# The first image's four chunks of x, loaded in halves of 64 channels instead of halves of 512 columns

## The chip, the core and the metric

The kernel runs on one core of one Trainium2 chip. The core has TensorE (matrix products, PE in the profile, with its weight loads shown apart as PEld), VectorE (DVE), ScalarE (ACT), GpSimd (POOL) and SyncE (SP, which here only issues transfers). Transfers between the memory of the chip (HBM) and the core's on-chip memory (128 partitions) are issued by SP, ACT or POOL, each on a queue of its own, and are carried out by 16 DMA engines that all queues share.

The metric is the time of one execution in microseconds on the device. The kernel before takes 3139.58 us, the median of three runs that lie between 3139.58 and 3139.60 us.

## What is computed

The input x has 16 images of 512 channels by 32 x 32 pixels, in float32. For every image: a group normalisation over 8 groups of 64 channels, a 1 x 1 convolution to queries, keys and values, attention with 4 heads of 128 channels over the 1024 pixels, a 1 x 1 convolution of the result, and the sum with x.

```python
b, c, h, w = x.shape                                   # 16, 512, 32, 32
xg = x.reshape(b, NUM_GROUPS, -1)                      # 8 groups
mu = jnp.mean(xg, axis=-1, keepdims=True)
var = jnp.var(xg, axis=-1, keepdims=True)
xn = ((xg - mu) * jax.lax.rsqrt(var + EPS)).reshape(b, c, h, w)
xn = xn * norm_gamma[:, None, None] + norm_beta[:, None, None]
qkv = jnp.einsum('oc,bchw->bohw', qkv_w, xn) + qkv_b[:, None, None]
q, k, v = jnp.split(qkv, 3, axis=1)
q, k, v = (to_heads(q), to_heads(k), to_heads(v))      # 4 heads of 128
attn = jax.nn.softmax(jnp.einsum('bhnd,bhmd->bhnm', q, k) * scale, axis=-1)
out = jnp.einsum('bhnm,bhmd->bhnd', attn, v)
out = out.transpose(0, 1, 3, 2).reshape(b, c, h, w)
out = jnp.einsum('oc,bchw->bohw', proj_w, out) + proj_b[:, None, None]
return x + out
```

## The kernel before, in words

An image is held as four chunks of 128 channels by 1024 pixels: the channels lie on the partitions, and a chunk is 512 KB. The products with the weights are done by Strassen's scheme (seven products of blocks instead of eight, for queries and keys on two levels), so that a chunk is used in blocks of 512 columns: b11 and b12 are the left and right halves of the upper two chunks, b21 and b22 those of the lower two. The images are pipelined: while the attention of one image runs, the statistics, the normalisation and the products of the next one are placed between its matrix products. Only the first image has nothing in front of it, and its work up to the first product is written out by hand in `open_image`.

The order at the start, by line:

- `load_x(0)` (L227 to L237, called at L240) issues the first transfers of the program. For each of the four chunks SP loads the left 512 columns and ACT the right 512 columns, so each queue issues four transfers of 128 rows of 2 KB. Images after the first are loaded by POOL, one transfer of 128 rows of 4 KB for each chunk.
- `stage_v` (L490 to L505) then makes SP load the weights of the values: a11, a21, a22 and a12, two transfers of 128 KB each. They use the same eight semaphores as the transfers of x, one after the other, so each of them is issued only when the x transfer that had its semaphore has landed. Further weights (`load_block`, L380; L434) follow on SP.
- TensorE starts with small products of constants (`warm`, L1263 to L1268) that no result uses. They stand at three places between the steps of the statistics.
- The statistics of the upper two chunks are made on VectorE (`chunk_steps`, L44 to L54): `bn_stats` (L49) of the left half, of the right half, and `bn_aggr` (L52). Two products with a matrix of averages (L82 and L87), some small steps on VectorE and a power on GpSimd (L89) give scale and shift for the groups of these two chunks (L76, L1293).
- Then the upper chunks are normalised in place, half by half (`apply`, L104 to L111): the left halves on VectorE (L111), the right halves on ScalarE (L108). The first product of the program's result, p1 of the values (`v_units`, L839 to L848), needs the left halves of both upper chunks and a11. Its result is copied by ScalarE (L565).
- ScalarE makes the statistics of the third chunk (L1303 to L1307) as soon as it is there, VectorE those of the fourth (L49 again). The lower chunks are normalised later (L1355 to L1358).
- The sums of the scheme follow on VectorE: t1 = b12 - b11 for each of the upper chunks and s1 = a21 + a22 (L1284), which the next product, p5, needs.

The instructions of the opening are kept in the order of the program where `keep_in_program_order` is called on them; the others are placed by a planner, which estimates when their operands are there.

Of the kernel before, what the change touches and what calls it, by code (L numbers as in the profile page):

```python
# [16 lines left out]
P = 128  # L17
# [4 lines left out]
HALF = 512  # L22
# [163 lines left out]
def fast_path(ctx, tc, x, sources, out, consts, flag, dims):  # L186
# [7 lines left out]
    B, C, N, NCC, NH2, NB, GC, SCALE = dims  # L194
# [29 lines left out]
    xs, xb, vs, qs, ks, os_, ob = {}, {}, {}, {}, {}, {}, {}  # L224
    mvs, scaled = {}, {}

    def load_x(b, chunks=range(NCC)):  # L227
        for c in chunks:
            xs[b, c] = xpool.tile([P, N], F32, tag="x", name=f"x_{b}_{c}")
            for half in range(NH2 if b == 0 else 1):  # L230
                i = ts(half, HALF) if b == 0 else ds(0, N)

                eng = nc.gpsimd if b > 0 else nc.scalar if half == 1 else nc.sync
                dma = eng.dma_start(xs[b, c][:, i], x[b, ts(c, P), i])
                if b > 0:

                    tc.keep_in_program_order(dma)  # L237


    load_x(0)  # L240
    primer = one.tile([BLK, 1], F32, name="primer")
    nc.vector.memset(ones, 1.0)
# [709 lines left out]
    def where(s):  # L952
        bh, j = divmod(s, NB)
        return (*divmod(bh, HEADS), j)
# [232 lines left out]
    def plan_head(b, h):  # L1187
# [3 lines left out]
        if h == 0:  # L1191
            if b > 0:
                products(plan, staggered(next_qk.pop()), NB)
                plan[6].append(lambda: o_blocks(b - 1))
                plan[6].append(lambda: sums_of_b(ob[b - 1]))
            else:
                products(plan, staggered(next_qk.pop(), (0, 4, 8, 12)), 0)
                plan[1].append(beside["second head"])
                plan[3].append(lambda: load_x(1, range(KC)))
                for c in range(KC):  # L1200
                    for half, step in enumerate(stats_steps(1, c)):
                        plan[4 + 2 * c].append(lambda step=step: behind_exp(step))
        elif h == 1:
            if b > 0:
                products(plan, staggered(proj_groups(b - 1), (0, 4, 8, 13)), NB, "proj")
            if b + 1 == B:
                plan[0].append(lambda: last_loads("x"))
            else:
                chunks = range(NCC) if b > 0 else range(KC, NCC)
                plan[0].append(lambda: load_x(b + 1, chunks))  # L1210
                at = (2, 4) if b > 0 else (1, 3)
                spread(plan, [lambda c=c: stats_chunk(b + 1, c) for c in chunks], *at)
                gather, scale = stats_group(b + 1)
                if b == 0:
                    plan[3].append(gather)
                    plan[4].insert(0, scale)
                else:
                    plan[4].insert(0, gather)
                    plan[5].insert(0, scale)
                for r in range(2):  # L1220
                    units = [
                        lambda c=c, half=half: normalise(b + 1, c, half, b > 0 or c % 2 == 1)
                        for c in range(KC * r, KC * r + KC) for half in range(NH2)
                    ]
                    plan[5 + r] += units if b > 0 else [
                        lambda u=u: behind_exp(u) for u in units
                    ]
                plan[6].append(lambda: x_sums(b + 1, (1,)))
# [159 lines left out]
    for s in range(steps + 1):  # L1388
        units = []
        if s < steps:  # L1390
            b, h, j = where(s)
# [175 lines left out]
```

## Time and profile before

| what | value |
|---|---|
| median of 3 runs | 3139.58 us (3139.58 to 3139.60) |
| the profiled execution | 3139.65 us |
| its span, first to last instruction | 3137.9 us |
| TensorE busy | 3129.2 us (100% of the span) |
| VectorE / ScalarE / GpSimd busy | 2658.0 / 1446.3 / 512.2 us |
| granted TensorE clock, mean over the span | 0.999 |
| issue of the eight x transfers of image 0 | 0.76 to 2.61 us |
| first product of the result (p1 of the values) | starts at 11.14 us |

Times within the profile are microseconds from the first instruction of the program. Busy time is the time in which an engine had an instruction under way. The chain that ended last follows the work back from the last instruction, at each step to what released it. A transfer is issued at one time and lands later; it has landed when all of its 16 parts have counted up its semaphore.

### The profile page before, as it was taken

The page shows a single profiled execution, that of the slowest core. Times are in us where ns is not written, and L with a number is a line of the kernel's source. Part 1 is how long each engine was busy: PE and PEld are TensorE (multiplying, and loading weights), DVE is VectorE, ACT ScalarE, POOL GpSimd, SP SyncE. Part 2 cuts the span into 40 slices and gives each one's busy share as a digit, 9 for nine tenths or more (in the row PEclk, how much of TensorE's full clock was granted, in tenths as well). Part 3 has the DMA queues.
Part 4 walks back from the last instruction along what each step waited for, and adds up shares of the span by engine and source line. Part 5 has one row for each costly group of instructions (what it writes and reads, how often), then busy time and mean ns, then how long its engine had stood idle before and what let it go on. Part 6 is the DMA issues. An engine that isn't in the chain of part 4 may idle for free.

```text
span 3137.9 us, 34036 instructions
## 1 busy us (share of the span) xinstructions
PE 3129.2 (100%) x10400; PEld 2197.3 (70%) x10400; DVE 2658.0 (85%) x4665; ACT 1446.3 (46%) x2653; POOL 512.2 (16%) x922
## 2 busy tenths in 40 slices
PE   9999999999999999999999999999999999999999
PEld 7567777777777777777777777777777777777764
DVE  8988889788897888978799787997879978799785
ACT  3545435354354543545435453453534545344433
POOL 0121121111211112111121101212012120121200
PEclk9999999999999999999999999999999999999999
DMA  5554554545545455454555545555455554555631
GB/s 177 169 193 148 197 172 165 164 152 191 172 169 165 146 198 172 162 168 148 194 170 170 169 143 189 174 172 172 142 183 172 178 183 134 183 162 182 191 118 48
DMA packets 209692, 522.21 MB, mean 166 GB/s; under 512 B 32336, under 2 KB 65488, under 8 KB 209504
## 3 DMA queue, kind: packets, MB, share of 16 engines
q1 hardware_dynamic: 131360, 277.34, 28.7%
q0 software_dynamic: 65184, 207.75, 19.5%
q10 hardware_dynamic: 12960, 34.87, 3.3%
q8 instruction: 86, 1.41, 0.2%
q14 instruction: 102, 0.84, 0.1%
HBM read 386.67 MB, written 133.17 MB: 166 GB/s over the span
## 4 chain that ended last, share of the span: by engine, by line
PE 100%; DMA 0%; DVE 0%; issue 0%; SPq 0%
PE po L1033 28%; PE s L960 28%; PE qk_x L687 12%; PE qk_y L687 9%; PE v_x L687 6%; PE pp_x L687 6%; PE pp_y L687 4%; PE v_y L687 4%; PE v_x L841 0%; PE lx L1119 0%; PE v_y L841 0%; PE ly L1119 0%; DMA x<-in_x 0%; PE v_z L841 0%; PE lz L1119 0%; PE warm L1267 0%
## 5 line engine op out<-in xcount | busy, mean ns | idle before, releaser
L960 PE MATMUL s<-qk,qk 128*128 128x512 f32 x2048 | 1045.9, 592 | 0.2 <-DVE qk L823 0.2
L1033 PE MATMUL po<-p,v 128*128 128x512 f32 x2048 | 1045.5, 592 | 0.0
L966 ACT ACTIVATE p<-s 128x512 f32<-128x512 f32 x1024 | 610.4, 596 | 877.7 <-PE s L960 859.2
L1033 PEld LDWEIGHTS po<-p,v 128*128 128x128 f32 x2048 | 616.3, 301 | 375.1 <-issue 258.0
L979 DVE TENSOR_TENSOR tot<-tot,p 128x1024 f32<-128x1024 f32 x385 | 469.4, 1219 | 142.2 <-ACT p L966 141.0
L960 PEld LDWEIGHTS s<-qk,qk 128*128 128x128 f32 x2048 | 389.0, 190 | 70.9 <-issue 14.6
L687 PEld LDWEIGHTS qk_x<-qk_t,w 128*128 128x128 f32 x1344 | 254.5, 190 | 153.3 <-issue 95.5
L687 PE MATMUL qk_x<-qk_t,w 128*128 128x256 f32 x1344 | 353.4, 380 | 0.0
L565 ACT COPY qk_u<-qk_x 128x512 f32<-128x512 f32 (+1 forms) x256 | 136.3, 532 | 238.0 <-PE qk_x L687 238.0
L892 POOL DMA_DIRECT2D vd<-vu x120 | 66.4, 553 | 958.9 <-DVE vu L884 958.9
L712 DVE TENSOR_TENSOR qk_r<-qk_y,qk_u 128x512 f32<-128x512 f32 (+1 forms) x256 | 157.7, 616 | 34.2 <-ACT qk_u L565 21.8
L943 POOL DMA_DIRECT2D out_y<-y x120 | 65.1, 543 | 645.5 <-DVE groups L300 401.3
L712 DVE TENSOR_TENSOR v_r<-v_y,v_u 128x512 f32<-128x512 f32 (+1 forms) x120 | 75.7, 631 | 107.7 <-ACT v_u L565 77.4
L687 PE MATMUL pp_x<-pp_t,w_proj 128*128 128x256 f32 x630 | 165.4, 379 | 0.0
L687 PE MATMUL v_x<-v_t,w_v 128*128 128x256 f32 x630 | 165.4, 379 | 0.0
L661 POOL DMA_DIRECT2D kept_t<-qk_t x240 | 129.6, 542 | 216.3 <-DVE qk_t L655 190.2
L687 PEld LDWEIGHTS pp_x<-pp_t,w_proj 128*128 128x128 f32 x630 | 119.7, 190 | 62.5 <-issue 35.9
L687 PEld LDWEIGHTS v_x<-v_t,w_v 128*128 128x128 f32 x630 | 119.7, 190 | 59.0 <-issue 34.4
L897 POOL DMA_DIRECT2D v<-vd x240 | 140.0, 590 | 65.5 <-issue 36.8
L687 PE MATMUL qk_y<-x,w 128*128 128x256 f32 x512 | 142.1, 379 | 0.0
L823 DVE SCALAR_TENSOR_TENSOR qk<-qk_r,qkb_sb,qk_r 128x512 f32<-128x512 f32 x192 | 137.4, 745 | 1.7
L884 DVE STREAM_TRANSPOSE vu<-vt 128x512 f32<-128x512 f32 x120 | 135.3, 1128 | 0.2 <-DMA vd<-vu 0.2
(229 smaller groups left out, 4395.1 us busy)
## 6 DMA issues: line engine op xcount, KB each, us to landing
w<-kept SPq DMA_DIRECT2D x90, 512.0 KB, 3.9
kept_t<-qk_t POOLq DMA_DIRECT2D x180, 256.0 KB, 2.7
v_t<-kept_t SPq DMA_DIRECT2D x180, 256.0 KB, 2.8
w<-kept SPq DMA_DIRECT2D x90, 384.0 KB, 3.4
rinv<-row ACTq DMA_DIRECT2D x63, 512.0 KB, 4.8
x<-in_x POOLq DMA_DIRECT2D x60, 512.0 KB, 4.8
vd<-vu POOLq DMA_DIRECT2D x120, 256.0 KB, 2.8
v<-vd POOLq DMA_DIRECT2D x240, 128.0 KB, 4.0
```

What stands on the lines that cost most here:

```text
L565: nc.scalar.copy(t[n][:, :width], t["x"][:, :width])
L661: nc.gpsimd.dma_start(t, to)
L687: latest["product"] = nc.tensor.matmul(acc[:, ts(i, Q)], have["w"][t][:, i, slot, :], inner(i, bn), start=(first and i == 0), stop=True, s ...
L712: latest["outer"] = nc.vector.tensor_add(dst, view(a), view(c))
L823: return nc.vector.scalar_tensor_tensor(st[b, h][:, ts(half, HALF)], a, qkb_sb[:, i : i + 1], c, ALU.add, ALU.add)
L884: nc.vector.transpose(u.rearrange("p (q i j) -> p j q i", q=n, i=BLK), t.rearrange("p (j q i) -> p j q i", q=n, i=BLK),)
L892: nc.gpsimd.dma_start(rows[which][ts(h, P), :], u)
L897: nc.gpsimd.dma_start(vs[b, pair][ts(q, BLK), half].rearrange("m h (k i) j -> m (h k) (i j)", k=n), rows[which].rearrange("(k m) (q e) -> ...
L960: latest["score"] = nc.tensor.matmul(sc, ks[b, h][:, ts(j, P)], qs[b, h][:, ts(half, HALF)], start=True, stop=True)
L966: exps[s] = nc.scalar.activation(ps[s][:, ts(half, HALF)], sc, AF.Exp, scale=SCALE)
L979: added[b, h, j] = nc.vector.tensor_add(tot[b, h][:, i], tot[b, h][:, i], ps[s][:, i])
L1033: summed = nc.tensor.matmul(po[half], v_block(b, h, j), ps[s][:, i], start=(j == 0), stop=(j == NB - 1),)
```

## The change

The transfers of image 0 are cut the other way: SP loads channels 0 to 63 of each chunk and ACT channels 64 to 127, all 1024 columns. Each queue still issues four transfers of 256 KB, now 64 rows of 4 KB on 64 partitions instead of 128 rows of 2 KB on 128 partitions. Images after the first are loaded as before.

```diff
             for half in range(NH2 if b == 0 else 1):
-                i = ts(half, HALF) if b == 0 else ds(0, N)
+                i = ts(half, P // 2) if b == 0 else ds(0, P)
 
                 eng = nc.gpsimd if b > 0 else nc.scalar if half == 1 else nc.sync
-                dma = eng.dma_start(xs[b, c][:, i], x[b, ts(c, P), i])
+                dma = eng.dma_start(xs[b, c][i, :], x[b, ts(c, P), :][i, :])
```

An instruction that reads a half of the columns of a chunk, on all 128 partitions, had one transfer to wait for and now has two. In the instruction streams this shows at the left-half `bn_stats` of the first, second and fourth chunk (L49), at the right-half normalisations on ScalarE (L108) and at the first products that read a chunk. The order of the instructions is the same on TensorE, VectorE, GpSimd and SP. On ScalarE one pair changes places: the copy of p1 (L565, `v_0_p`) now stands ahead of the normalisation of the second chunk's right half (L108) instead of behind it:

```
 L108 Activation x_0<-x_0,sh,sc 128x512
+L565 TensorCopy v_0_p<-v_0_x 128x512
 L108 Activation x_1<-x_1,sh,sc 128x512
-L565 TensorCopy v_0_p<-v_0_x 128x512
 L565 TensorCopy v_1_p<-v_1_x 128x512
```

## The prediction

> **What bounds the kernel now.** I read the page first, then the chain that ended last in its first 16 us, then the waits, the stretches and the transfers there. The page:
>
> ```profile
> PE 3129.2 (100%) x10400; PEld 2197.3 (70%) x10400; DVE 2658.0 (85%) x4665; ACT 1446.3 (46%) x2653; POOL 512.2 (16%) x922
> PE 100%; DMA 0%; DVE 0%; issue 0%; SPq 0%
> ```
>
> TensorE is busy from end to end and is the chain. The change leaves its 10400 products alone, so the end can only move if the first real product (p1, line 841) starts at another time, or if TensorE later waits. What sets p1 is the opening (start us, length us, what):
>
> ```profile
> 0.76 0.39 SPq L234
> 1.15 0.06 issue
> 1.21 4.83 DMA x<-in_x
> ...
> 6.06 1.30 DVE st L49 x2
> ...
> 7.38 0.22 DVE mv L52
> ...
> 7.64 0.40 PE pm L82 x2
> ...
> 8.66 0.38 PE pv L87 x2
> 9.05 2.12 PE warm L1267 x18
> 11.16 2.41 PE v_x L841 x10
> ```
>
> The chain begins with the second chunk's left-half transfer, which lands at 6.03; the statistics start at 6.06, the average at 7.64. From 9.05 to 11.14 TensorE is filled with products of constants, but the real chain there is ve, the power on GpSimd, scale, shift and the normalisation (VectorE, to 11.09), after which p1 starts at 11.14. So what the second chunk gains or loses at 6.06 goes 1:1 to p1, and as TensorE is never idle after it, 1:1 to the end.
>
> A second chain ends close by: p1 needs a11, which SP loads behind x.
>
> ```profile
> SPq L503 <- DMA x<-in_x: 4.1, 4, 1.9
> DVE st L49 <- DMA x<-in_x: 3.1, 2, 2.9
> ACT junk L1303 <- DMA x<-in_x: 3.7, 1, 3.7
> ```
>
> By the trace's landings, the SP transfers of x land at 4.32, 6.03, 7.61 and 8.97, ACT's at 4.49, 6.22, 7.86 and 9.16; a11 lands at 9.44 and 9.81 (1.3 us before p1), a21 and a22 by 11.25 (their sum s1 starts at 13.71). How busy the transfers are, by stretch (last column GB/s):
>
> ```profile
> 4.50:6.00 1.50, 1.50 (x15) 1.50 (x15) 1.34 (x3) 0.00 (x0) 0.00 (x0) 1.00 1.02 378
> 6.00:7.50 1.50, 0.28 (x3) 0.09 (x1) 1.41 (x3) 0.00 (x0) 0.00 (x0) 1.00 1.06 396
> ```
>
> All 16 engines are full (share 1.02 and 1.06), so x arrives at the engines' rate and any change of that rate shows.
>
> **The change, part by part.**
>
> *Issue.* The eight transfers take 0.39 to 0.45 us each to issue. Transfers with 128 contiguous rows of 4 KB took 0.32 us (weights from the kept store, line 425) to 0.36 us (last image's x, line 1085). So 0.06 to 0.1 us less ahead of each; the second chunk's landing is set by the engines, so I count 0.07 us once at most.
>
> *Larger packets.* Packets of 2048 bytes take 84 ns on an engine, packets of 4096 bytes 159 ns (the trace's medians on the hardware queues). Up to the second chunk each engine moves 32 of the small ones, 2.69 us, or 16 of the large, 2.54 us: 0.14 us earlier if nothing else changes.
>
> *Waiting for both halves.* The first statistics of a chunk now need both transfers. For the second chunk the later one counts: 6.22 instead of 6.03, so +0.19 us. For the first chunk 4.49 instead of 4.34: its statistics would end at 6.03 instead of 5.88, just ahead of the second's start, nothing. These three together: 6.22 - 0.14 = 6.08, or 6.01 with the faster issue, against 6.03: -0.02 to +0.05 us.
>
> *64 partitions per transfer.* The trace has no 64-partition transfer of this kind. The nearest rows are the value blocks v<-vd, 128 KB onto 32 partitions each. In 245 to 246 us they run alone:
>
> ```profile
> q0 software_dynamic: 78, 0.20, 95.7%
> v<-vd POOLq DMA_DIRECT2D x3, 128.0 KB, 4.7
> ```
>
> 95.7% of 16 engines over 1 us is 15.3 us; less the 29 small packets at 9 ns each, 49 packets of 4 KB took 307 ns each, nearly twice 159, and 0.20 MB a us is half of the 378 to 396 GB/s above. Landings of these blocks come 0.7 us apart, those of the 128 KB weight transfers onto 128 partitions 0.36 us. Part of it may be their 512-byte pieces (27 ns each, eight make 216 ns), so the row bounds the cost from above. From below: here two queues work on the two disjoint halves at once, and engines that take turns could keep all partitions busy, which costs nothing (159 ns). I take the middle, 1.5 x 159 = 239 ns: both queues begin together, 0.2 us apart at most, so the engines start in step on the same half, but nothing holds them in step.
>
> The landing of chunk c (0 to 3) is 0.76 + 2.39 + 8 p (c + 1), p the packet time; 2.39 us is what the first chunk shows over its sixteen 84 ns packets (4.49 - 0.76 - 1.34). The next chunk came 0.39 us later than this rule; at the slower rate I let that be absorbed.
> - p = 159 ns: as computed above, 6.08.
> - p = 239 ns: second chunk 6.97, fourth 10.8. Statistics start at 7.0 instead of 6.06: +0.95. a11's first piece comes 0.28 us behind ACT's fourth transfer (9.44 - 9.16), so 11.1, its second 0.37 later; p1 at 12.1. The weights are no bound.
> - p = 318 ns: second chunk 8.24, +2.2 by the statistics; fourth 13.3, a11 at 13.6 and p1 there: +2.5. Now the weights set it.
>
> *Clock.* TensorE idles from 6.29 to 7.64 now (1.36 us) and keeps the clock. At the end of the program the last product ends at 3132.40 and the recorded clock halves at 3134.53, after 2.1 us. With +0.95 the gap is 2.3 us, so the clock may halve before line 82; at the start it took from 1.45 to 4.51 to be granted in full. The 22 constant products would then run at 213 instead of 112 ns, and would still be running when p1 is ready: line 82 at 8.6, full clock at about 11.7, by then 8 of the last 18 are done, the other 10 take 1.1 us, p1 at 12.8 instead of 12.1. Between 0 and +0.7 us; I take 0, since both times are near the edge.
>
> *SP, ACT and what stands behind.* SP's weight transfers wait for the x landings and come later by what x loses (fourth chunk +1.6 at 239 ns, +4.1 at 318): a22 at 11.25 + 4.1 = 15.4 against s1 at 13.71 + 2.5 = 16.2, covered; the query weights land by 16.65 and are read at 25.25, covered. ScalarE's copy of p1 now stands ahead of the second chunk's right half: that normalisation moves from 11.3 to 13.77 and ends at 14.55, while its reader t1 starts at 14.84 after other VectorE work. Free, with 0.3 us of cover; VectorE would pass any overrun to p5 (14.98) 1:1, bounded by the 0.58 us of the copy. The additional waits on PE, DVE and ACT are a semaphore instruction each (17 ns where the trace shows them), on queues that stand idle then.
>
> *Sum.* Profiled execution 3139.65 (span 3137.9 and 1.75 around it), 0.07 us over the median: 3139.58 + 0.95 + 0.0 (issue, packets and both halves are inside the landings) + 0 (clock) = 3140.5 us.
>
> **The rivals.**
>
> A. *The halves overlap in full* (p = 159 ns): -0.02 to +0.05 us, 3139.6 us; at best 3139.4, if packets and issue gain and ACT's half no longer trails. For it: the two queues together cover all 128 partitions. Against it: v<-vd.
>
> B. *The halves take turns* (p = 318 ns): +2.5 us and up to +0.9 for the clock, whose gap is then 3.5 us: 3142.1 to 3143.0. For it: v<-vd at 307 ns. [...]
>
> C. *Slower by more than 0.2%, through a11.* p1 waits for a11, which queues on SP behind x. This decides from p1 = 11.14 + 6.3 = 17.4, a11 at 17.4 and the fourth chunk at 17.1: p = (17.1 - 3.15) / 32 = 436 ns, 2.7 times the row of 159 and 1.4 times the slowest sustained row (307). With B's clock at half for three more microseconds of products (+1.5) it is 3144.5, still inside. Single 4 KB packets over 436 ns exist, only beside other queues' traffic. Time: 3146 and more.
>
> D. *Faster by more than 0.2%* would need 6.3 us of the 11.14 before p1; x would have to land before it is issued. Practically out.
>
> **How the numbers follow.** 0.2% (6.3 us) is about what a measurement can tell from no change. Middle case 0.38, A 0.29, B 0.27, C 0.05, D 0.01. The likeliest is the middle, 3140.5. The range runs from A's best, 3139.4, to B with its clock, 3143.0, and leaves out C, D and little else. Faster 0.01, slower C's 0.05 and 0.01 for what B might add; the rest, 0.93, is within 0.2%.
>
> **What would show it.** Second chunk's statistics starting at about 7.0 (A: 6.05, B: 8.3); packets of 4 KB on the SP and ACT queues at 240 ns (159, 318); DMA rate in 4.5 to 7.5 us near 270 GB/s (390, 205); p1 at 12.1 (11.1, 13.7), released by VectorE's normalisation in the middle case, by a11 in B; t1 of the second chunk still right behind its VectorE predecessor. I am wrong if p1 moves by over 0.3 us while the packets stay at 159 ns, or if the end moves otherwise than p1.

## The result, and the profile after

The changed kernel takes 3144.17 us (median of 22 runs, 3142.93 to 3145.12) against 3139.62 us for the kernel before (22 runs, 3139.42 to 3140.24): a ratio of 1.0014, 95% interval 1.0008 to 1.002. That is 4.5 us slower, within the 0.2% named in the prediction, but outside its range, which ended at 3143.0. The profiled execution took 3144.00 us with a span of 3142.2 us (before 3139.65 and 3137.9).

The page shows the same bound as before; TensorE's 10400 products take 2.8 us more:

```profile
PE 3132.0 (100%) x10400; PEld 2200.2 (70%) x10400; DVE 2658.4 (85%) x4665; ACT 1446.1 (46%) x2653; POOL 512.3 (16%) x922
```

The chain that ended last in the changed kernel, first 18 us (start us, length us, what):

```profile
0.76 0.60 SPq L234
1.36 0.06 issue
1.42 6.67 DMA x<-in_x
...
8.18 1.30 DVE st L49 x2
...
9.76 0.59 PE pm L82 x2
10.35 1.06 PE warm L1267 x4
11.41 0.22 PE pv L87 x2
11.63 4.05 PE warm L1267 x18
15.68 2.29 PE v_x L841 x10
```

The statistics of the second chunk start at 8.18 instead of 6.06 us (+2.12). But p1 starts at 15.47 instead of 11.14 (+4.33; the chain's 15.68 is the end of the last constant product). So more than half of the loss does not come from the late x. Two things lie between. The first normalisation (line 111) starts at 13.13 instead of 10.54, that is +2.59: the two averaging products (0.59 instead of 0.40 us, and one that has to wait for the constant products ahead of it) cost 0.47 us. The normalised half is there at 13.68, and a11 landed at 12.27 and 12.60, yet the 18 constant products take 4.05 instead of 2.12 us and occupy TensorE until 15.5: another 1.74 us. The sum 2.12 + 0.47 + 1.74 is 4.33. The last product of the program ends at 3136.67 instead of 3132.39, +4.28: nothing is won back or lost later.

Why the constant products are slow is seen in stretches of 3.41 us, cut at the recorded changes of the clock (5.58, 8.99 and 15.82 us) and once between them (busy us of PE, PEld, DVE, ACT, POOL with counts, then the granted TensorE clock, DMA share, GB/s):

```profile
2.17:5.58 3.41, 3.41 (x18) 3.41 (x17) 0.00 (x0) 1.49 (x2) 0.36 (x1) 1.00 1.02 245
5.58:8.99 3.41, 1.22 (x11) 1.02 (x9) 2.31 (x5) 0.00 (x0) 0.00 (x0) 1.00 1.06 242
8.99:12.41 3.42, 2.65 (x12) 2.65 (x13) 1.39 (x7) 1.33 (x3) 0.49 (x1) 0.50 1.04 288
12.41:15.82 3.41, 3.41 (x17) 3.40 (x16) 3.00 (x9) 1.97 (x4) 2.10 (x4) 0.50 1.02 287
15.82:19.23 3.41, 3.41 (x18) 3.00 (x17) 2.03 (x8) 1.30 (x2) 0.00 (x0) 1.00 0.85 229
```

TensorE was idle from 6.79 to 9.76. The clock was halved at 8.99 and came back only at 15.82, two stretches of 3.41 us later. In the kernel before, stretches of the same length, cut from its recorded change at 4.51 us, give:

```profile
1.09:4.51 3.42, 3.06 (x14) 3.06 (x15) 0.39 (x3) 1.49 (x2) 1.22 (x2) 1.00 0.71 218
4.51:7.92 3.41, 2.05 (x19) 1.86 (x17) 2.82 (x6) 0.04 (x1) 0.00 (x0) 1.00 1.04 385
7.92:11.33 3.41, 3.32 (x26) 2.96 (x27) 1.84 (x10) 3.34 (x7) 2.00 (x4) 1.00 1.00 319
```

There TensorE was busy for 60% of the stretch with the gap, and the clock stayed. (The first rows of both tables show 1.00 because no clock is recorded before its first change; the first products there run 213 ns apart, as at the granted 0.50, against 112 ns after the change.)

The last column tells of the transfers: 242 to 245 GB/s while x is loaded, against 385 before, with all engines full in both (share 1.02 to 1.06). Packets of 4 KB took 262 ns (SP) and 265 ns (ACT) in the mean, 260 and 250 in the median; in the kernel before, packets of 4 KB on these queues took 159 in the median.

### The profile page after: what moved, and what is told of

It is laid out like the page before. It is cut to its first block, busy times and chain, and to the rows that moved or that the text cites. A ratio compares the mean times of both kernels' runs of the same rounds, so it can differ in the third digit from the quotient of the medians.

```text
span 3142.2 us, 34045 instructions
## 1 busy us (share of the span) xinstructions
PE 3132.0 (100%) x10400; PEld 2200.2 (70%) x10400; DVE 2658.4 (85%) x4665; ACT 1446.1 (46%) x2653; POOL 512.3 (16%) x922
## 4 chain that ended last, share of the span: by engine, by line
PE 99%; DMA 0%; DVE 0%; SPq 0%; issue 0%; DVEq 0%
PE po L1033 28%; PE s L960 28%; PE qk_x L687 12%; PE qk_y L687 9%; PE v_x L687 6%; PE pp_x L687 6%; PE pp_y L687 4%; PE v_y L687 4%; PE v_x L841 0%; PE lx L1119 0%; PE v_y L841 0%; PE ly L1119 0%; DMA x<-in_x 0%; PE warm L1267 0%; PE v_z L841 0%; PE lz L1119 0%
## 5 line engine op out<-in xcount | busy, mean ns | idle before, releaser
L565 ACT COPY qk_u<-qk_x 128x512 f32<-128x512 f32 (+1 forms) x256 | 136.3, 532 | 238.0 <-PE qk_x L687 238.0
```

Of the source, the lines that this page charges most:

```text
L565: nc.scalar.copy(t[n][:, :width], t["x"][:, :width])
```

## The experiments

My theory after this result: x comes about 2 us late, because transfers onto 64 adjacent partitions are slow and start late, and any such delay costs the clock on top. The rivals: the late x alone makes the 4.5 us; or it is rows of 4 KB, 64 rows, or the two queues, and not the partitions.

**Alternate channels.**

```diff
-                i = ts(half, P // 2) if b == 0 else ds(0, P)
+                i = ds(half, P // 2, 2) if b == 0 else ds(0, P)
```

> The changed kernel, but SP takes the even channels of each chunk and ACT the odd ones, instead of the lower and the upper 64: the same 64 rows of 4 KB per transfer on the same queues, spread over all 128 partitions. If the cause is that a transfer lies on 64 adjacent partitions: packets near 160 ns, the second chunk's statistics at 6.0 to 6.4 us, 3139.4 to 3139.9 us. If 64 rows of 4 KB are slow in themselves (issue of 0.6 us, few rows for each engine, late first packet): packets of 250 ns and more, statistics near 8.2 us, 3143 to 3145 us as for the changed kernel. If the issue alone stays long (0.6 us) and the packets recover: statistics near 6.5 us, 3140.0 us.

Measured: 3142.27 us (3140.63 to 3144.09; before in the same job 3139.78). The packets recover: median 159 ns on both queues, all of x landed by 10.02 instead of 12.08. But the start does not, and the total missed what I had written for each of the three cases. The issue in this run:

```profile
L234 SPq DMA_DIRECT2D x<-in_x x4: 594/606/825, 0.8 to 2.9; - x4
L234 ACTq DMA_DIRECT2D x<-in_x x4: 565/612/618, 0.8 to 2.6; - x4
```

Min, median and max in ns: 0.6 us, as in the changed kernel, against 0.39 to 0.45 before. ACT's first packet starts at 2.12 and SP's at 3.25 us (before 1.98 and 1.78). The second chunk's statistics start at 7.34, between the cases, and the clock halved from 9.35 to 12.77; p1 came at 13.61. So adjacency makes the packets slow, and something else makes the start late. Alternate channels also lie 8 KB apart in HBM, where the changed kernel reads 64 channels in one piece; no run tells the two sides apart, but the next run reads 512 KB in one piece and is fast.

**Whole chunks on one queue.**

```diff
-            for half in range(NH2 if b == 0 else 1):
-                i = ts(half, P // 2) if b == 0 else ds(0, P)
+            for half in range(1):
+                i = ds(0, P)
```

> Each chunk of the first image in one transfer of 128 rows of 4 KB, all four on SP, none on ACT. If 64 adjacent partitions are the cause: packets of 4 KB at 159 ns, second chunk's statistics at 5.9 to 6.2 us, 3139.4 to 3139.8 us. If rows of 4 KB are the cause: packets of 250 ns, statistics near 8 us, 3143 us or more. If a single queue cannot fill the 16 engines: statistics near 7 us, 3140.5 us.

Measured: 3139.51 us (3139.41 to 3139.82), ratio to the kernel before 0.9999, interval 0.999 to 1.0008. Rows of 4 KB are not slow on 128 partitions (packets of 159 ns in the median, 179 in the mean), and one queue fills the engines. The transfers in 4.5 to 7.5 us of this run (packets, MB, share of 16 engines), and its chain:

```profile
q1 hardware_dynamic: 321, 1.18, 100.0%
```

```profile
0.76 3.78 DMA x<-in_x
4.54 0.02 issue
4.56 1.30 DVE st L49 x2
...
6.09 1.16 DVE st L49 x2
```

The second chunk lands at 5.80, but its statistics wait for VectorE to finish the first chunk's: p1 at 11.04. The runs lie a little below those of before, and the interval does not tell them apart.

**The clock kept by more constant products.**

```diff
-        warm(14, "warm_0")
+        warm(26, "warm_0")
```

> The changed kernel with 26 instead of 14 products of constants ahead of the first average (line 82), so that TensorE is busy until about 9.2 us; x arrives as in the changed kernel. If the halved clock adds about half of the 4.5 us: the clock stays full, the average still starts near 9.8 us, p1 at 13.7 instead of 15.5 us, 3142.0 to 3142.4 us with runs closer together than the 3142.9 to 3145.1 of the changed kernel. If the late x alone makes the 4.5 us: no change, 3144.2 us.

Measured: 3142.72 us (3142.17 to 3144.41). TensorE in this run:

```profile
1.45 8.40 PE L1267 MATMUL warm<-avg 128*128 128x128 f32 x52 [1.45 <-DVE avg L247]
9.75 0.38 PE L82 MATMUL pm<-mv,avg 128*128 128x2 f32 x2
9.99 0.69 PE L1267 MATMUL warm<-avg 128*128 128x128 f32 x4
10.78 0.38 PE L87 MATMUL pv<-vv,avg 128*128 128x2 f32 x2
11.02 2.25 PE L1267 MATMUL warm<-avg 128*128 128x128 f32 x18
13.26 0.92 PE L841 MATMUL v_x<-wv,x 128*128 128x256 f32 x3
```

x is as late as in the changed kernel (statistics at 8.17), the clock stays full from 6.36 on, and p1 starts at 13.26: +2.12 over before, the delay of x and nothing more. With x equally late, p1 is 2.2 us earlier than in the changed kernel. The total fell by 1.45 us in the median, less than p1; in the profiled execution 0.4 us went between p1 and the last product (3121.6 against 3121.25 us), 0.34 us of it at one product of queries and keys that waited for VectorE (47.32 us, line 712), and 0.4 us behind the last product, which I did not follow. Two of the eleven runs were at 3144.4. They have no profile; their mean granted clock is 0.999, where eight of the other nine have 1.0, so 26 products do not keep the clock in every run, it seems.

**Both halves on one queue.**

```diff
-                eng = nc.gpsimd if b > 0 else nc.scalar if half == 1 else nc.sync
+                eng = nc.gpsimd if b > 0 else nc.sync
```

> The changed kernel with both halves of every chunk on SP, one behind the other. If a transfer onto 64 adjacent partitions runs at half rate by itself: packets near 310 ns, 2.5 us or more per chunk, the second chunk's statistics at 8.5 to 9.5 us, 3144 to 3146 us. If the two queues hinder each other and one half alone is fast: packets near 160 ns, statistics near 6.5 us, 3140 us.

Measured: 3143.54 us (3143.00 to 3144.64), a little less than I expected for half rate. Packets take 298 ns in the median and 291 in the mean; the chunks are complete at 5.82, 8.24, 10.55 and 12.84 us, 2.34 us apart. In the changed kernel, with two queues, they are complete at 5.74, 8.09, 10.96 and 12.08, 2.11 apart. So transfers onto one half are slow on a single queue too, and a second queue with the other half wins 11%. In the kernel before, chunks come 1.56 us apart.

**Late x in the old form.**

```diff
+    early = rpool.tile([P, 2, 2, HALF], F32, tag="r0", name="early").rearrange(
+        "p a b m -> p (a b m)"
+    )
+    for half, eng in enumerate((nc.sync, nc.scalar)):
+        eng.dma_start(early[:, ds(half * N, 768)], x[1, ts(half, P), 0:768])
     load_x(0)
```

> The kernel before, with one more transfer of 384 KB (128 rows of 3 KB, read by nobody) ahead of x on each of the two queues. x then comes about 2.1 us later through unchanged transfers. If any delay of x of that size costs itself and the clock: second chunk's statistics at 8.1 to 8.5 us, the clock halved in most runs, 3142.5 to 3145 us, spread over 1 us and more. If only the delay counts: 3141.7 to 3142.1 us with close runs. If the 4.5 us belong to the form of the transfers: under 3141 us.

Measured: 3144.42 us (3143.32 to 3144.86; before 3139.79), the same as the changed kernel. Its chain:

```profile
1.20 6.43 DMA x<-in_x
...
8.59 1.28 DVE st L49 x2
...
10.15 0.59 PE pm L82 x2
10.74 1.06 PE warm L1272 x4
11.80 0.22 PE pv L87 x2
12.02 4.03 PE warm L1272 x18
```

The second chunk's statistics start 2.5 us late, a little later than I had planned. The clock is halved from 9.08 to 15.90, the constant products take 4.03 us, and p1 starts at 15.86, 4.7 us late. Transfers of the old form that are late do the same kind of damage as the new ones.

**An idle TensorE with x on time.**

```diff
-        warm(14, "warm_0")
+        warm(4, "warm_0")
```

(in the kernel before)

> The kernel before with 4 instead of 14 products of constants ahead of the first average; x is on time. If an idle TensorE there is what halves the clock: average at 7.64 us as before, but the 18 constant products behind it run at half clock, p1 at 12.0 to 13.2 us, 3140.5 to 3141.8 us. If the clock costs nothing while no real product runs: 3139.6 to 3139.9 us.

Measured: 3141.24 us (3140.89 to 3142.78). The average runs at 7.46, earlier than before, but the clock is not granted until 13.81, and p1 starts at 13.17 (11.14 before):

```profile
3.57:6.99 3.42, 0.00 (x0) 0.00 (x0) 2.48 (x5) 0.56 (x2) 0.00 (x0) 1.00 1.02 374
6.99:10.40 3.41, 2.94 (x14) 2.95 (x15) 1.11 (x8) 2.42 (x5) 0.79 (x2) 1.00 1.03 345
10.40:13.81 3.41, 3.41 (x16) 3.32 (x16) 3.27 (x9) 1.70 (x4) 1.80 (x3) 1.00 0.83 235
```

(The clock column is again unrecorded before its first change.) So the clock alone costs 1.45 us in the median, without any late transfer; every run lies above all those of the kernel before.

**Rows of 2 KB, and 32 rows,** one execution each, without an interval. In the first, every transfer of the changed kernel is cut into two of 512 columns, in the second into two of 32 adjacent channels.

```diff
+            for part in range(4 if b == 0 else 1):
+                half, side = divmod(part, 2)
+                j = ts(side, HALF) if b == 0 else ds(0, N)
...
+                dma = eng.dma_start(xs[b, c][i, j], x[b, ts(c, P), :][i, j])
```

> The changed kernel with each transfer cut once more, in two of 512 columns: 64 rows of 2 KB on 64 adjacent partitions, eight on each queue. If 64 rows in a transfer make the issue long: 0.6 us each again; if it was the 4 KB rows: 0.4 us. If adjacent partitions set the packet time: packets of 2 KB at 130 to 160 ns instead of 84, second chunk at 8 to 9 us, 3143 us or more; else 84 ns and 3140.5 us.

```diff
+            for part in range(4 if b == 0 else 1):
+                half = part // 2
+                i = ts(part, P // 4) if b == 0 else ds(0, P)
```

> The changed kernel with each transfer cut once more, in two of 32 rows of 4 KB on 32 adjacent partitions. If fewer rows make the issue longer: over 0.6 us; if it goes with the rows to be written down: about 0.3 us. Packets of 250 to 310 ns if 64 and 32 adjacent partitions are alike, second chunk at 8 to 9 us, 3143 us or more; 500 ns and later than 10 us if 32 are half as fast as 64.

Measured, 64 rows of 2 KB: 3142.84 us; the first eight issues 0.6 us, packets 105 ns in the median and 116 to 123 in the mean (84 and 90 to 96 in the old form), less than I expected; statistics of the second chunk at 7.57, p1 at 13.8. So adjacency costs less with rows of 2 KB (105 against 84 ns) than with rows of 4 KB (250 to 260 against 159). Measured, 32 rows of 4 KB: 3141.55 us; issues of 0.40 to 0.44 us at the start, packets 254 and 259 ns, so 32 adjacent partitions are like 64. Here the second chunk is complete at 7.30, earlier than the 8 to 9 us I expected and 0.79 us ahead of the changed kernel although the packets are as slow. I put this down to the issue and the first packets (SP 1.79 and ACT 2.54 us here, 3.02 and 2.15 there); that the transfers are smaller was not tested apart. The clock stayed in this run, and p1 came at 12.58, exactly as much later (+1.43) as the statistics (7.49 against 6.06).

**32 rows, spread.**

```diff
-                i = ts(part, P // 4) if b == 0 else ds(0, P)
+                i = ds(part, P // 4, 4) if b == 0 else ds(0, P)
```

> The run with 32 rows of 4 KB per transfer, but with every fourth channel in a transfer instead of 32 adjacent ones, so that each transfer is spread over all 128 partitions. If the 0.6 us issue goes with 64 rows and the slow packets with adjacent partitions, both are gone: issue near 0.4 us, packets near 160 ns, second chunk's statistics at 6.0 to 6.6 us, 3139.5 to 3140.2 us. If adjacency is not what slows the packets: 250 ns, statistics near 7.5 us as with adjacent rows, 3141.5 us.

Measured: 3142.72 us (3140.88 to 3144.46; before 3139.61). The packets are at 159 ns in the median, as expected, but the issue is 0.59 us again, so the long issue does not go with 64 rows: it is there for 64 adjacent, 64 alternate and 32 spread partitions, and not for 32 adjacent or all 128. The first chunk is complete only at 5.94, VectorE makes its statistics first, and the second chunk's start at 7.56 although it is there at 6.87. The clock halved from 11.02 to 14.43, and p1 came at 13.84. I had expected 3139.5 to 3140.2.

**Fewer constant products behind the second average.**

```diff
-            warm(9, "warm_2")
+            warm(4, "warm_2")
```

> The changed kernel with 4 instead of 9 products of constants behind the second average (line 87). If these products at half clock hold back p1, which is ready near 13.7 us: p1 at 13.6 to 13.9 us, but real products then run at half clock until the clock returns, 0.5 to 1.5 us less than the changed kernel, 3142.7 to 3143.7 us. If p1 waits for x or a11: p1 at 15.5 us, 3144.2 us.

Measured: 3144.16 us (3141.70 to 3145.35), no gain in the median, where I expected 0.5 to 1.5 us.

```profile
11.57 2.06 PE L1267 MATMUL warm<-avg 128*128 128x128 f32 x8
13.81 3.58 PE L841 MATMUL v_x<-wv,x 128*128 128x256 f32 x10 [0.18 <-DVE x L111]
```

p1 does start at 13.8, released by the normalisation: the constant products were what held it. But the first ten real products then take 3.58 us instead of 2.43, since the clock returns only at 16.18. In the profiled execution the last product ends 0.52 us earlier than in the changed kernel; over the runs nothing is left.

## Why the prediction was wrong

**What held.** TensorE remained the chain, p1's delay went 1:1 to the end (4.33 against 4.28 us), and the delay began at the second chunk's statistics. The cover of the later steps held too: a22 landed at 14.07 against s1 at 16.30, and ScalarE's copy ahead of the second chunk's right half cost 0.16 us of VectorE's time (t1 at 18.91, waiting for ScalarE), which p5 did not feel, though the prediction would have passed it on 1:1 (p5 starts 3.86 us after p1, before 3.84). The weights did not bind: a11 landed at 12.27, before p1 was ready. The direction was right.

**The step "64 partitions per transfer" was sized too small.** I took 239 ns, the middle between 159 and 318; 262 to 265 ns were measured in the mean, between the middle and the v<-vd row (307) that I had called a bound from above. (That row was itself a little high: in the mean its small packets took 17 ns, not 9, and its 4 KB packets 302.) By the formula of the prediction that is 0.4 us at the second chunk. The middle between two far rows had no row of its own behind it.

**The step "Issue" had the wrong sign.** I expected 0.06 to 0.1 us less for each transfer; the issue became 0.2 us longer, and the first packets came 0.2 (ACT) and 1.2 us (SP) later. I also let the 0.39 us by which the second chunk had come later than the formula be absorbed. Together 0.73 us: 3.15 + 16 x 0.263 = 7.36, landed 8.09. The run with 32 adjacent rows, with the old issue and nearly the same packets, bears it out: 7.30. The statistics so started 2.12 us late where the sum had 0.95.

**The step "Clock" was taken at 0 and measured 2.2 us at p1.** This is the largest term (p1 at 15.47 against 13.26 with the clock kept and x equally late; 1.45 us in the median of the runs). I saw that the gap would come near the 2.1 us after which the clock had halved at the end, and gave the return of the clock 3 us of work, as at the start. Both are wrong as rules. The recorded changes of the clock lie on a grid: 5.58, 8.99 and 15.82 us in the changed kernel, one step of 3.413 and one of 6.827 us. In these runs it went roughly by how busy TensorE was in the stretch before: 36% (the changed kernel) halved the clock, 60% (the kernel before) did not; 78% (the changed kernel) and 86% (the run with 4 constant products) did not bring it back, 90% (the kernel before) did. But between 36% and 60% the busy share did not decide. These are the stretches ahead of a grid point with alternate channels, with 32 adjacent rows and with 32 rows spread:

```profile
5.94:9.35 3.41, 1.46 (x12) 1.27 (x12) 2.31 (x7) 0.00 (x0) 0.00 (x0) 1.00 1.00 356
5.11:8.53 3.42, 1.46 (x13) 1.27 (x12) 2.54 (x5) 0.86 (x1) 0.00 (x0) 1.00 1.06 257
7.61:11.02 3.41, 1.95 (x14) 1.60 (x14) 2.15 (x8) 3.33 (x6) 0.19 (x1) 1.00 0.85 262
```

The first (43%) and the third (57%) were followed by half clock, the second (43%) was not. In that run the idle gap of 2.50 us lies across the grid point at 8.53, and the clock stayed; that may have been luck. What decides it stays open. In the changed kernel, a clock lost at 8.99 with work from 9.76 on did not return at 12.41, and the 22 constant products, meant to keep TensorE warm, ran at some 220 ns each and stood in front of p1.

**Scatter.** The grid is not tied to the start of the program: its points (recorded changes, or 3.41 us from one) are 5.58 and 8.99 us in the changed kernel, 5.11 and 8.53 with 32 adjacent rows, 5.94 and 9.35 with alternate channels. That fits the runs: 3139.42 to 3140.24 before, but two groups, 3142.9 to 3143.5 and 3144.0 to 3145.1, after. The profiled execution belongs to the upper group. The mean granted clock of each run, rounded to a thousandth, goes with the groups: 0.999 in all nine runs of the lower, 0.998 in nine of the thirteen of the upper. With alternate channels the four fastest runs (3140.6 to 3141.1 us) have 1.0 and the two slowest (3143.5 and 3144.1) 0.998. So the late x leaves more or less half clock from run to run; that the place of the grid is the reason is argued, not shown.

**The rivals.** B came nearest: its second chunk at 8.24 against 8.09, in part by chance, since its packets were too slow (318 ns) and its start too early; its clock was +0.9 instead of 2.2, and a11, which was to set p1, did not. The 3144.5 us that the prediction works out under C, for B with three more microseconds at half clock, would have covered the result, but the range stopped at 3143.0. A rested on two queues that together cover all partitions; they win only 11% over one (2.11 us a chunk against 2.34). C and D did not come near.

Left open: why some forms of a transfer take 0.6 us to issue and send their first packet late (128 partitions do neither, 32 spread, 64 adjacent and 64 alternate do both; 32 adjacent are issued in 0.4 us, but ACT's first packet came late there too, at 2.54). No run here tells it apart.

## What to carry to other kernels

Cut a load that must be early by columns, or not at all, and give every transfer a row on each of the 128 partitions; a single queue with whole chunks was as fast as two queues here (3139.51 us, and 3139.62 by columns; 3144.17 by 64 adjacent partitions, 3142.27 by 64 alternate ones). When the first operand of a TensorE-bound kernel comes later, count the delay and then the clock: here 2.12 us of delay, with TensorE idle for 2.97 us, cost another 2.2 us at p1. Remember that filler products at half clock stand in front of the real ones (18 of them took 4.05 us instead of 2.12). A term that is "near the edge" belongs in the range at its full price, not at zero.

## What the runs showed of the hardware

- Packets of 4 KB, in the mean: 179 ns on an engine onto 128 partitions on one queue (whole chunks), 254 to 259 ns onto 32 adjacent partitions, 262 to 265 ns onto 64 with two queues (the changed kernel) and 291 ns with one.
- Partitions with a step of 2 (alternate channels) or 4 (32 rows spread) gave 159 ns in the median again (171 to 223 in the mean), as on 128 partitions, without using all 128 in one transfer.
- The time to issue a transfer did not go with its rows: 0.6 us for 64 rows of 4 KB or 2 KB and for 32 spread rows, 0.4 us for 32 adjacent rows and for 128.
- The recorded changes of TensorE's clock lay 3.41 us apart (alternate channels, 32 rows spread), 6.82 us (late x) or both (the changed kernel): an idle gap of 2.97 us (the changed kernel) went with 6.83 us of half clock, one of 1.36 us (the kernel before) with none. Length alone did not decide: one of 2.50 us (32 adjacent rows) also went with none, one of 1.37 us (32 rows spread) with 3.41 us of half clock.
